# Blocks 0 to 2 of a four-block model in one structure with one set of PSUM banks, with the work between the attentions issued as steps among them

## The chip, the cores and the metric

The kernel runs on one core of one Trainium2 chip. The metric is the device time of one execution in microseconds. Before the change it is 3795.54 us, the median of three runs (3782.44 to 3795.83). The program is written in a tile language: the author allocates named tiles in pools, and a scheduler at build time gives them addresses, adds the semaphore waits and fixes the order of the instructions on each engine by its own estimate and by priority, which is the order in the program text. Where a matmul is pinned (`keep_in_program_order`), TensorE issues it in the order of the text.

## The reference, cut to what matters

Four residual blocks follow each other on x, of shape [4 batches, 1024 tokens, 128 channels]. Each computes `xn = layernorm(x); s = attn(xn); g = silu(ffn(xn)); x = x + s * g`.

- Block 0: attention of 16 heads of size 8 with rotary positions and a window of 250 keys; as ffn an RWKV channel mix: two blends of each token with the one before it, `r = sigmoid(xr @ W_r)`, `k = relu(xk @ W_k)**2`, `ffn = r * (k @ W_v)`.
- Block 1: causal attention; as ffn a mixture of 8 experts of which each token keeps its best two, hidden size 256, with gelu. All experts are computed for all tokens, and gates that are zero or not weigh them.
- Block 2: a whole transformer layer as attention (layernorm, full attention with rotary positions, `x + attn`, layernorm, an FFN of hidden size 512 with relu); as ffn a mixture of 8 experts of which each token uses one, with at most 80 tokens per expert over the whole input, so the place of a token among its expert's tokens depends on all batches.
- Block 3: a Mamba-like layer as attention and two layers of local attention as ffn. The change leaves its arithmetic alone.

Everything in blocks 0 and 1 and in block 2's attention is independent between the four batches. Only block 2's routing and its experts see all batches at once.

## The kernel before, in words

x, the normed x and s lie in SBUF as 32 tiles of 128 tokens (`k.x`, `k.xn`, `k.s`), and the normed x also turned, channels by tokens (`k.xT`). `tile_blocks` calls `_block0`, `_block1`, `_block2` and `_block3` one after the other. Each of the first three opens PSUM banks of its own by `_banks`, once for the norms, once for the attention and once for the ffn, and does each phase for all four batches before it goes on:

1. `_ln_to_fm` (L549): layernorm of a batch (`_layernorm_parts`: statistics and scaling on VectorE, the power -0.5 on GpSimd, L72) and eight transposes on TensorE (L88), for four batches.
2. `_attention` (L121). A unit is one batch and four heads, 16 units in all. `project` computes q and k, applies rotary positions, splits them in three bf16 parts on GpSimd (`_split`, L104 to L107) and stores them to DRAM; `load` reads them back in another layout (q9, k9). `maxima` computes all scores once to get each row's maximum: a matmul into `max_ps` and a reduction on VectorE (L288). `attend` computes the scores again into `sc`, applies exp on ScalarE (L363), masks on GpSimd where needed (L332), and multiplies by the values into `o_ps`. Its PSUM set is two pairs of banks (tag "m": projections, `max_ps`), three single banks (tag "s": `sc` and all transposes) and one bank (tag "o": `o_ps`).
   The order of work is written out by hand. Before the first `attend`, batch 0 is projected, units 0 and 1 are loaded, the maxima of unit 0 are taken and the first two fifths of those of unit 1. Then, for each unit, `_interleave` mixes as streams the maxima of the coming units, the blocks of this unit's `attend`, and a third of the projections of the next batch. All TensorE work here is pinned.
3. The ffn for all batches: the channel mix in L580 to L604; the router, the gates and the experts of block 1 in L640 to L690, with all expert weights resident; in block 2 the FFN (L745 to L772) and `_experts` (L817: a one-hot matrix per tile, dispatch matmuls, experts, combine).
4. `silu`, `g = s * g` on GpSimd (L98) and `x += g` on VectorE (L99).

All loads and stores are issued by SyncE in one in-order queue; an issue that waits holds up those behind it. Block 3's first weights (`_weights3`) are loaded into a pool on the right side of SBUF that is opened before block 2.

Of the kernel before, what the change touches and what calls it, by code (L numbers as in the profile page):

```python
# [29 lines left out]
P = 128  # L30
# [18 lines left out]
@contextmanager  # L49
def _banks(k):  # L50

    with k.tc.tile_pool(name="ps", bufs=2, space=PSUM) as k.ps:
        yield


# [26 lines left out]

def _to_fm(k, src, dst, scale=None, bias=None):

    nc, n = k.nc, src.shape[1]
    ps = k.ps.tile([P, 4, P], F32, tag="mx", name="tr_ps")
    for i in range(n):
        nc.tensor.transpose(ps[:, i, :], src[:, i, :], k.ident)  # L88
    flat = ps[:, :n, :].rearrange("p a b -> p (a b)")
    if scale is None:  # L90
        nc.scalar.copy(dst, flat)
    else:
        nc.vector.tensor_scalar(dst, flat, scale, bias, ALU.mult, ALU.add)


def _add_product(k, s, g, x):

    k.nc.gpsimd.tensor_tensor(g, s, g, ALU.mult)  # L98
    k.nc.vector.tensor_tensor(x, x, g, ALU.add)  # L99
# [10 lines left out]
def _interleave(*streams):  # L110

    total = max(len(s) for s in streams)
    done = [0] * len(streams)
    for step in range(total):
        for i, s in enumerate(streams):
            while done[i] < len(s) and done[i] * total < (step + 1) * len(s):
                s[done[i]]()
                done[i] += 1


def _attention(k, pool, mode, xT, w, out, rope=None):  # L121
# [22 lines left out]
    ps2 = lambda name: k.ps.tile([P, 2, 512], F32, tag="m", name=name, bufs=2)  # L144
    ps1 = lambda name: k.ps.tile([P, 512], F32, tag="s", name=name, bufs=3)
    pin = k.tc.keep_in_program_order

    def matmul(*args, **kw):
        pin(nc.tensor.matmul(*args, **kw))  # L149

    def transpose(*args):
        pin(nc.tensor.transpose(*args))

    def project(b):
# [5 lines left out]
        def half(what, hf):  # L160
            cols = slice(512 * hf, 512 * hf + 512)

            def step():
# [22 lines left out]
                if hf == 1:  # L186
                    parts = pool.tile([P, 3, T], BF16, tag="parts", name=f"{what}p", bufs=2)
                    _split(nc, nc.gpsimd, d, parts, d)
                    dense[what, "parts"] = parts
# [50 lines left out]
    def maxima(n):  # L240

        q9, k9 = units[n]
        neg = pool.tile([P, 4, NT], F32, tag="neg", name="neg", bufs=3)

        def tile_of(parts):


            def step():
                ps = ps2("max_ps")
# [51 lines left out]
        held = {}  # L301

        def split():
            held["p"] = parts = pool.tile([P, 3, 4 * NT], BF16, tag="negp", name="negp", bufs=2)
# [3 lines left out]
        def spread():  # L308
            parts = held.pop("p")
            tp = k.ps.tile([12 * NT, P], BF16, tag="s", name="neg_ps", bufs=3)  # L310
# [31 lines left out]
    def attend(n):  # L342
# [5 lines left out]
        def weights(hf, n):  # L348
            kt, c0, width = blocks[hf][n]
            off = kt * P - c0  # L350
            held[hf, n] = pt = pool.tile([P, 4, 384 if mode == "window" else 512], F32, tag="pt", name="pt", bufs=1 + lag)

            def pair(p2):
                for j in (2 * p2, 2 * p2 + 1):
# [8 lines left out]
                    nc.scalar.activation(pt[:, j, :width], sc[:, :width], AF.Exp, scale=scale)  # L363


                two = slice(2 * p2, 2 * p2 + 2)
                if mode != "full" and off >= 0:
                    keep(pt[:, two, off : off + P], 1, 0)
                edge = max(0, off + CONTEXT)
                if mode == "window" and width > edge:  # L370
                    keep(pt[:, two, edge:width], -1, off + CONTEXT - 1 - edge)
# [3 lines left out]
        def values(hf, n):  # L375
# [6 lines left out]
            o, pt = held["o", hf], held.pop((hf, n))  # L382
            for j in range(4):
# [4 lines left out]
                    rhs=pt[:, j, :width],  # L388
# [9 lines left out]
        def normalize(hf):  # L398
            os = held.pop(("os", hf))
            ot = k.ps.tile([P, 4, 4, 32], F32, tag="s", name="ot", bufs=3)  # L400
# [62 lines left out]

    def run(steps):
        for step in steps:
            step()

    run(project(0))
    load(0)
    load(1)  # L470
    steps, ending = maxima(0)
    run(steps + ending)
    steps, ending = maxima(1)
    lead = 2 * len(steps) // 5
    run(steps[:lead])
    late = []
    for n, (b, g) in enumerate(order):
        if g == 0:
            dense["at", b] = pool.tile([P, NT, H, HD], F32, tag="at", name="at", bufs=2)
        ahead = []  # L480
        if n + 1 < N:

            ahead = steps[lead:] + ending[:1]
            last = ending[1]
            if n + 2 < N:
                load(n + 2)
                steps, ending = maxima(n + 2)
                ahead += steps[: lead - 2] + [last] + steps[lead - 2 : lead]
            else:
                ahead.append(last)  # L490
        weights, closing = attend(n)
        streams = [ahead, weights]
        if b + 1 < B and g < 3:
            if g == 0:
                coming = project(b + 1)
            streams.append((coming[:3], coming[3:7], coming[7:])[g])
        if late:

            for i in range(lag + 1):
                weights.insert(1 + 2 * i, late[i])  # L500
            for i, step in enumerate(late[lag + 1 :]):
                weights.insert(min(len(weights), 2 * lag + 4 + 3 * i), step)
        _interleave(*streams)
        late = closing + (finish(b) if g == 3 else [])
    run(late)


def _first_max(k, pool, lg, name):

    nc = k.nc  # L510
    full = [P, NTILE, E8]
    m = pool.tile([P, NTILE, 1], F32, tag="fm_m", name="fm_m")
# [5 lines left out]
    i = pool.tile([P, NTILE, 1], F32, tag="fm_i", name="fm_i")  # L518
# [6 lines left out]
def _softmax8(k, pool, lg, m, scale):  # L525

    nc = k.nc
    full = [P, NTILE, E8]
# [3 lines left out]
    z = pool.tile([P, NTILE, 1], F32, tag="sm_z", name="sm_z")  # L532
# [6 lines left out]
def _router(k, pool, xT, wg, bg):  # L539

    nc = k.nc
    ps = k.ps.tile([P, NTILE, E8], F32, tag="ms", name="rt_ps", bufs=1)
    for n in range(NTILE):
        b, t0 = n // NT, 1 + (n % NT) * P
        nc.tensor.matmul(ps[:, n, :], lhsT=xT[:, b, t0 : t0 + P], rhs=wg, start=True, stop=True)
    lg = pool.tile([P, NTILE, E8], F32, tag="lg", name="lg")
    nc.vector.tensor_tensor(lg, ps, bg.unsqueeze(1).to_broadcast([P, NTILE, E8]), ALU.add)
    return lg


def _ln_to_fm(k, pool, src, xT, keep=None, scale=None, bias=None):

    for b in range(B):
        if keep is None:
            xn = pool.tile([P, NT, C], F32, tag="ln_x", name="ln_x", bufs=2)
        else:
            xn = keep[:, b * NT : b * NT + NT, :]
        _layernorm(k, src[:, b * NT : b * NT + NT, :], xn)
        for i in range(2):
            c0 = 1 + 512 * i  # L560
            _to_fm(k, xn[:, 4 * i : 4 * i + 4, :], xT[:, b, c0 : c0 + 512], scale, bias)


def _block0(k, t):
    nc = k.nc
    x, xT, s, g = k.x, k.xT, k.s, k.xn
    with k.tc.tile_pool(name="w0", bufs=1) as wp:
        w0 = wp.tile([P, 9 * P + 2], F32, name="w0")
        nc.sync.dma_start(w0, t["w0"])
        names = ("q", "qs", "k", "ks", "v", "o", "wr", "wk", "wv")  # L570
        w = {n: w0[:, i * P : i * P + P] for i, n in enumerate(names)}
        mu_r, mu_k = w0[:, 9 * P : 9 * P + 1], w0[:, 9 * P + 1 : 9 * P + 2]
        with k.tc.tile_pool(name="a0", bufs=1) as pool:
            rope = pool.tile([P, 2, T], F32, name="rope")
            nc.sync.dma_start(rope, t["rope"][:, 0])
            with _banks(k):
                _ln_to_fm(k, pool, x, xT)
            with _banks(k):
                _attention(k, pool, "window", xT, {n: w[n] for n in names[:6]}, s, rope)
        with k.tc.tile_pool(name="f0", bufs=2) as pool, _banks(k):  # L580
            for n in range(8):
                b, o = n // 2, 512 * (n % 2)
                cur, prev = xT[:, b, o + 1 : o + 513], xT[:, b, o : o + 512]
                dx = pool.tile([P, 512], F32, name="dx")
                nc.gpsimd.tensor_tensor(dx, cur, prev, ALU.subtract)
                xr = pool.tile([P, 512], F32, name="xr")
                nc.vector.scalar_tensor_tensor(xr, dx, mu_r, prev, ALU.mult, ALU.add)
                xk = pool.tile([P, 512], F32, name="xk")
                nc.vector.scalar_tensor_tensor(xk, dx, mu_k, prev, ALU.mult, ALU.add)
                kp = k.ps.tile([P, 512], F32, tag="ms", name="kp", bufs=1)  # L590
                nc.tensor.matmul(kp, lhsT=w["wk"], rhs=xk, start=True, stop=True)
                ka = pool.tile([P, 512], F32, name="ka")
                nc.scalar.activation(ka, kp, AF.Relu)
                nc.gpsimd.tensor_tensor(ka, ka, ka, ALU.mult)
                rv = k.ps.tile([P, 2, 4, P], F32, tag="sc", name="rv")
                for c in range(4):
                    cs = slice(c * P, c * P + P)
# [1234 lines left out]
```

## Time and profile before

The profiled execution took 3796.72 us; its trace spans 3795.0 us. The median of the three other runs is 3795.54 us, so a sum made on the trace is 1 to 2 us short of either.

| engine | busy in the span | instructions |
|---|---|---|
| TensorE, matmuls (PE) | 3349.1 us, 88% | 25426 |
| TensorE, weight loads (PEld) | 1858.6 us, 49% | 25428 |
| VectorE (DVE) | 2502.8 us, 66% | 4932 |
| ScalarE (ACT) | 1966.8 us, 52% | 4192 |
| GpSimd (POOL) | 1362.9 us, 36% | 1887 |

The mean granted TensorE clock is 0.916. The DMA queue of SyncE carries 118.98 MB; its packets take 13.7% of the 16 DMA engines' time. The profile's chain of work that ended last reaches back only to about 2750 us, into block 3, so it says nothing on the blocks before it.

How to read it: busy shares over the whole span average stages with different limits. The stages here can be cut by the first and last matmul of a kind. First scores of an attention: 104, 678 and 1655 us; last output projection: 533, 1221 and 2484 us; first matmul of block 3: 2744 us. A window table by these cuts, with each engine's busy time and the granted clock, is what the prediction works on. A fp32 matmul appears as two instructions.

### The profile page before, as it was taken

Reading aid. Unit: us, or ns where it says so; the run is one execution under the profiler, and the core shown is the slowest. Engines: PE = TensorE matmul, PEld = TensorE weight load, DVE = VectorE, ACT = ScalarE, POOL = GpSimd, SP = SyncE. Lnnn points to the kernel's source line nnn. Section 1 sums busy time; section 2 is a strip of 40 time slices with the busy share of each in tenths; the row PEclk is TensorE's granted clock in tenths of the full one; section 3 lists DMA queues with packets and bytes.
Section 4 is the critical chain, followed back from the end, with each engine's and each line's share of the span. In section 5 each row is a group of like instructions: output and inputs, shape, how many; then the busy total and the mean of one; then the engine's idle time right before and its main releaser. Section 6 shows DMA issues by size and latency. Waiting matters only on the chain. (4 is left out here: it accounts for less than half of the span.)

```text
span 3795.0 us, 65266 instructions
## 1 busy us (share of the span) xinstructions
PE 3349.1 (88%) x25426; PEld 1858.6 (49%) x25428; DVE 2502.8 (66%) x4932; ACT 1966.8 (52%) x4192; POOL 1362.9 (36%) x1887
## 2 busy tenths in 40 slices
PE   3999984999999999389999999989779999999898
PEld 2554542444444676123333233257756676666665
DVE  5666655777773434388778688444478888877785
ACT  0444551566565443036666666731056656665674
POOL 3555463322321001421110300010186677656663
PEclk7999995999998998579999999999589999999999
DMA  3222202212220000201111111010021001001110
GB/s 81 62 63 56 51 3 68 56 40 43 56 39 15 1 1 13 56 19 35 35 34 26 30 26 26 1 51 6 17 61 21 18 21 29 20 21 22 28 27 22
DMA packets 110419, 123.14 MB, mean 32 GB/s; under 512 B 77336, under 2 KB 89888, under 8 KB 102432
## 3 DMA queue, kind: packets, MB, share of 16 engines
q1 hardware_dynamic: 110112, 118.98, 13.7%
q8 instruction: 201, 3.29, 0.4%
q14 instruction: 106, 0.87, 0.1%
HBM read 77.91 MB, written 23.07 MB: 27 GB/s over the span
## 5 line engine op out<-in xcount | busy, mean ns | idle before, releaser
L363 ACT ACTIVATE pt<-sc 128x512 f32<-128x512 f32 (+3 forms) x2432 | 1073.1, 512 | 856.5 <-PE sc L149 848.2
L288 DVE TENSOR_REDUCE neg<-max_ps 128x1 f32<-128x1024 f32 (+6 forms) x1088 | 1171.5, 1102 | 485.2 <-PE max_ps L149 469.1
L149 PE MATMUL max_ps<-k,q 72*128 72x512 bf16 (+3 forms) x2304 | 683.0, 366 | 140.1 <-DMA k<-kx 104.7
L149 PE MATMUL sc<-q,k 75*128 75x512 bf16 (+3 forms) x2432 | 646.8, 343 | 45.9 <-ACT pt L363 35.0
L149 PE MATMUL o_ps<-pt,va 128*32 128x512 f32 (+3 forms) x4864 | 561.8, 528 | 4.6 <-POOL pt L332 4.4
L332 POOL TENSOR_SCALAR_AFFINE_SELECT pt<-pt 128x256 f32<-128x256 f32 (+2 forms) x768 | 290.6, 394 | 512.1 <-ACT pt L363 506.1
L149 PEld LDWEIGHTS <-q 72*128 72x128 bf16 x2304 | 227.4, 101 | 413.1 <-issue 289.7
L149 PEld LDWEIGHTS <-k 75*128 75x128 bf16 x2432 | 183.0, 98 | 496.6 <-issue 399.2
L104 POOL CAST negp<-neg 128x32 bf16<-128x32 f32 x48 | 10.0, 209 | 643.8 <-DVE neg L288 643.7
L1384 ACT ACTIVATE pr<-lsc,nb,r 128x128 f32<-128x128 f32 x512 | 202.2, 475 | 62.1 <-DVE nb L1376 58.6
L1305 POOL TENSOR_TENSOR qn<-qn,rot 128x512 f32<-128x512 f32 x128 | 164.5, 1291 | 137.3 <-DVE rot L1297 122.6
L1314 POOL TENSOR_TENSOR rn<-ss,neghalf 128x16 f32<-128x16 f32 x64 | 188.8, 2949 | 69.7 <-DVE ss L1312 60.2
L149 PEld LDWEIGHTS o_ps<-pt,va 128*32 128x32 f32 x4864 | 100.9, 109 | 204.8 <-issue 162.1
L149 PEld LDWEIGHTS <-ident 128*128 128x128 bf16 x1472 | 151.8, 104 | 89.0 <-issue 23.8
L679 PEld LDWEIGHTS op<-ew,h 128*128 128x128 f32 x1024 | 134.1, 195 | 66.5 <-ACT h L675 34.8
L675 ACT ACTIVATE h<-hp,eb 128x512 f32<-128x512 f32 x128 | 87.5, 687 | 133.9 <-PE hp L668 133.9
L688 DVE SCALAR_TENSOR_TENSOR xn<-op,gates,xn 128x128 f32<-128x128 f32 x256 | 72.0, 344 | 125.0 <-PE op L679 122.7
L1222 PE MATMUL qk_ps<-wqkv,hT 128*128 128x512 f32 x256 | 135.2, 612 | 21.7 <-DVE hT L1268 7.3
L679 PE MATMUL op<-ew,h 128*128 128x128 f32 x1024 | 138.4, 279 | 4.6 <-ACT h L675 4.6
L149 PE MATMUL max_ps<-mask_window,ident 128*128 128x134 bf16 (+2 forms) x960 | 139.2, 228 | 0.0
L668 PE MATMUL hp<-xT,ew 128*128 128x512 f32 x256 | 134.5, 608 | 0.4 <-ACT h L675 0.4
L395 DVE COPY os<-o_ps 128x512 f32<-128x512 f32 x96 | 65.5, 682 | 85.3 <-PE o_ps L149 85.3
(355 smaller groups left out, 5742.4 us busy)
## 6 DMA issues: line engine op xcount, KB each, us to landing
q<-qx SPq DMA_DIRECT2D x144, 192.0 KB
k<-kx SPq DMA_DIRECT2D x432, 64.0 KB
va<-vb SPq DMA_DIRECT2D x120, 128.0 KB
qx<-qp SPq DMA_DIRECT2D x12, 768.0 KB
kx<-kp SPq DMA_DIRECT2D x12, 768.0 KB
mw<-in_e2w_dram SPq DMA_DIRECT2D x2, 2048.0 KB
q<-negr SPq DMA_DIRECT2D x144, 8.0 KB
x<-in_x_dram SPq DMA_DIRECT2D x4, 512.0 KB
```

The lines of the kernel that those rows point to most:

```text
L149: pin(nc.tensor.matmul(*args, **kw))
L288: nc.vector.tensor_reduce(neg[:, j0 : j0 + m, qt0], of, AX.X, ALU.max, negate=True)
L332: nc.gpsimd.affine_select(out=pt, in_=pt, pattern=[[0, 2], [step, pt.shape[2]]], compare_op=ALU.is_ge, fill=0.0, base=base, channel_multip ...
L363: nc.scalar.activation(pt[:, j, :width], sc[:, :width], AF.Exp, scale=scale)
L668: nc.tensor.matmul(hp[:, hh, :], lhsT=ew1[:, e, hh * P : hh * P + P], rhs=xT[:, b, o : o + 512], start=True, stop=True,)
L675: nc.scalar.activation(h[:, hh, :], hp[:, hh, :], AF.Gelu, bias=eb1[:, e, hh : hh + 1])
L679: nc.tensor.matmul(op[:, c, :], lhsT=h[:, hh, c * P : c * P + P], rhs=ew2[:, e, hh, :], start=hh == 0, stop=hh == 1,)
L688: nc.vector.scalar_tensor_tensor(to, op[:, c, :], gates[:, 4 * n + c, e : e + 1], to, ALU.mult, ALU.add)
L1222: pin(nc.tensor.matmul(*args, **kw))
L1305: nc.gpsimd.tensor_tensor(qn[:, i], qn[:, i], rot, ALU.add)
L1314: nc.gpsimd.tensor_tensor(rn, ss.rearrange("p w h -> p (w h)"), k.neghalf[:, : 2 * NH], ALU.pow)
L1384: nc.scalar.activation(t.pr[:, h, :], t.sc[r][:, c, :], AF.Exp, bias=t.nb[r][:, c : c + 1], scale=t.r8[:, h : h + 1])
```

## The change

- One function `_blocks012` holds blocks 0 to 2 with one PSUM pool that is open throughout: the attention's set ("m", "s", "o"). All other matmuls of the three blocks up to block 2's FFN use its tags and are pinned in program order too (helpers `_mm`, `_tr`, `_ps1`, `_ps2`).
- `_attention` no longer runs by itself. It returns `begin`, a list of steps up to the first `attend`, and `rest(post, aside)`. `rest` runs the units and has one more stream, `aside`: `post(b-1)` gives the steps that follow batch b-1's attention, and they are spread over the units 1 to 3 of batch b. What `post` gives for the last batch is returned.
- The phases became lists of small steps per batch or half batch: `_norm_steps`, `_fm_steps`, `_update_steps`, `_channel_mix`, `_silu_steps`, `_moe`, `_gating`, `_ffn`. They are placed so: the norms of batches 1 to 3 and the whole channel mix beside block 0's `begin`; x update, norm, router and gates of block 1 for batches 0 to 2 inside block 0's attention; those of batch 3 and the experts of block 1 for batches 0 to 2 beside block 1's `begin`; x update, norm, router logits and second norm of block 2 for batches 0 to 2 inside block 1's attention; the experts for batch 3 beside block 2's `begin`; batch 3's update and norms and the FFN of batches 0 to 2 inside block 2's attention; the FFN of batch 3 after it, then block 2's routing, then the experts as before.
- The exp tile `pt` is allocated per pair of heads (five buffers of two heads, tag "pt") instead of per block (2 or 3 buffers of four heads), and other steps take their scratch from the same five buffers; `ln_x` and `fm` share the two buffers of tag "os".
- Block 1's expert weights are no longer resident: `fetch(e)` loads one expert's 256 KB, for each batch anew, into three rotating buffers, from the SyncE queue.
- Block 2's expert weights are loaded after its attention as before, but the FFN of only one batch lies between. `_weights3` moved behind blocks 0 to 2.

The diff, cut to its core:

```diff
             def pair(p2):
+                held[hf, n, p2] = pt = pool.tile([P, 2, 512], F32, tag="pt", name="pt", bufs=5)
...
+    begin = project(0) + [lambda: load(0), lambda: load(1)] + steps + ending
+    begin += steps[:lead]
+    def rest(post, aside=[]):
...
+            if b and g == 1:
+                aside += post(b - 1)
+            share = -(-len(aside) // (4 - g))
+            if share and (b == 0 or g):
+                streams.append(aside[:share])
+                aside = aside[share:]
+            _interleave(*streams)
+            late = closing + (finish(b) if g == 3 else [])
+        _run(late)
+        return post(B - 1)
+    return begin, rest
...
+def _moe(k, pool, wp, t, gates, eb1, eb2, b):
+    def fetch(e):
+        ews[e] = ew = wp.tile([P, 512], F32, tag="ew", name="ew", bufs=3)
+        nc.sync.dma_start(ew[:, 0:256], t["e1w1"][:, e])
+        nc.sync.dma_start(ew[:, 256:512].rearrange("p (h c) -> p h c", h=2), t["e1w2"][:, e])
...
+    for i in range(len(jobs) + 1):
+        if i < len(jobs):
+            e, n = jobs[i]
+            if n == 0 and e + 2 < E8:
+                steps.append(lambda e=e: fetch(e + 2))
+            steps.append(lambda e=e, n=n: hidden(e, n))
+        if i:
+            steps.append(lambda i=i: output(*jobs[i - 1]))
...
+def _ffn(k, pool, w, b):
+    def output(n, f2):
+        h = held.pop(("h", n, f2))
+        if f2 == 0:
+            held["op", n] = _ps1(k, "op2", (P, 4, P))
...
+    steps = [lambda: nc.gpsimd.tensor_tensor(s[:, a, :], s[:, a, :], k.xn[:, a, :], ALU.add), None]
+    for i in range(2):
+        steps += [lambda i=i: norm(i), None, lambda i=i: held.pop(("n", i))(), lambda i=i: to_fm(i)]
...
+                begin, rest = _attention(k, pool, "window", xT, wa, s, rope)
+                _run(normed[0])
+                mix = [_channel_mix(k, pool, w, mu_r, mu_k, n) for n in range(2 * B)]
+                for b in range(B):
+                    other += (normed[b + 1] if b + 1 < B else []) + mix[2 * b] + mix[2 * b + 1]
+                _interleave(other + _silu_steps(k, range(B)), begin)
+                last = rest(lambda b: to_block1(b, wp, wp))
...
+        begin, rest = _attention(k, pool, "causal", xT, wa, s)
+        _interleave(moe(pool, 0) + moe(pool, 1) + moe(pool, 2), last, begin)
+        last = rest(lambda b: to_block2(b, pool) if b < B - 1 else [])
...
+        begin, rest = _attention(k, pool, "full", xT, wb, s, rope)
+        _interleave(moe(pool, B - 1), begin)
+        _run(rest(lambda b: _ffn(k, pool, wb, b), to_block2(B - 1, pool)))
...
-    _block0(k, t)
-    _block1(k, t)
+    _blocks012(k, t, lambda b: _norm3(k, b))
+    stream.close()
     with tc.tile_pool(name="early3", bufs=1, side="right") as wp:
         _weights3(k, t, wp)
-        _block2(k, t, lambda b: _norm3(k, b))
-        stream.close()
         _block3(k, t, out)
```

## The prediction

> **What bounds the kernel now.** I read the slices first, then a window table cut by stages, then TensorE's waits in the stages with low busy time, then the groups of instructions for durations. In the slices, the digits under PE and the granted clock fall together at the joints between the attentions:
>
> ```profile
> PE   3999984999999999389999999989779999999898
> PEclk7999995999998998579999999999589999999999
> ```
>
> The second view is the window table (us, busy of PE, PEld, DVE, ACT, POOL, then clock, DMA share, GB/s):
>
> ```profile
> 0.00:104.00 104.00, 43.57 (x202) 27.48 (x202) 56.16 (x133) 7.14 (x11) 36.73 (x37) 0.76 0.33 79
> 104.00:533.00 429.00, 394.60 (x3593) 215.65 (x3591) 259.10 (x368) 216.29 (x646) 235.18 (x596) 0.96 0.24 51
> 533.00:678.00 145.00, 74.51 (x320) 46.24 (x321) 90.54 (x168) 32.22 (x41) 62.91 (x41) 0.62 0.21 50
> 678.00:1221.00 543.00, 516.57 (x3775) 222.00 (x3774) 371.52 (x473) 333.31 (x780) 154.67 (x340) 0.98 0.19 40
> 1221.00:1655.00 434.00, 346.78 (x1699) 229.99 (x1698) 192.60 (x585) 120.48 (x169) 65.05 (x43) 0.79 0.08 20
> 1655.00:2484.00 829.00, 795.05 (x4341) 255.72 (x4340) 607.36 (x661) 549.14 (x1048) 107.14 (x125) 0.98 0.12 25
> 2484.00:2744.00 260.00, 229.72 (x1188) 184.00 (x1187) 113.25 (x283) 41.25 (x98) 33.73 (x26) 0.79 0.06 25
> 2744.00:3795.00 1051.00, 948.26 (x10318) 677.52 (x10320) 812.24 (x2266) 667.00 (x1400) 667.52 (x679) 0.95 0.11 27
> ```
>
> I call the rows A (start), B (window attention), C (joint), D (causal attention), E (joint), F (full attention), G (block 2's FFN and experts) and H (block 3). In B, D and F TensorE is busy 92 to 96% at clock 0.96 to 0.98. That this is its peak shows in the timeline of F: a block of `attend` with its maxima takes 2.83 us, and its matmuls start every 0.22 us without a gap, while DVE waits 0.48 us per block for `max_ps`. So in B, D and F every matmul put in costs its own time, and other engines have room. In A, C and parts of E TensorE waits. The third view cuts E and G finer:
>
> ```profile
> 1234.00:1487.00 253.00, 245.72 (x1378) 174.96 (x1377) 101.47 (x360) 108.30 (x150) 11.97 (x6) 0.97 0.00 1
> 1487.00:1546.00 59.00, 32.50 (x135) 25.77 (x133) 37.32 (x170) 7.23 (x11) 11.02 (x7) 0.53 0.06 20
> 1546.00:1601.00 55.00, 11.77 (x33) 6.01 (x34) 2.17 (x9) 4.95 (x8) 39.94 (x25) 0.59 0.27 75
> 1601.00:1655.00 54.00, 44.57 (x90) 11.21 (x89) 50.66 (x45) 0.00 (x0) 0.91 (x4) 0.50 0.20 38
> 2485.00:2565.00 80.00, 72.47 (x369) 50.78 (x370) 35.43 (x87) 21.88 (x32) 16.55 (x13) 0.89 0.15 60
> ```
>
> The experts of block 1 (first row) are bound by TensorE: 253 us for 8 half batches, 31.6 us each. Then come 59 us of update, norms and routing, 55 us in which GpSimd prepares q and k and TensorE does nearly nothing, and 54 us of first maxima bound by DVE. The fourth view names the waits of E:
>
> ```profile
> PE max_ps L149 <- DMA k<-kx: 42.7, 1, 42.7
> PE tr_ps L88 <- DVE ln_x L76: 22.0, 6, 7.0
> ```
>
> **The change part by part.** TensorE's work stays: both programs have the same number of matmuls. What can go is waiting and half clock at the joints. I place the moved work with the built program's order of instructions, which has no times.
>
> A, 104 us. Batch 0's projection no longer waits for the transposes of four batches (it starts at 37.4 us now), but on GpSimd the five memsets (3 x 3.5 and 2 x 1.2 us) now stand ahead of the first norm's power (first issued at 7.7 us now, then about 17), and five blends, two squares and two or three powers (1.0 to 1.4 us each) stand inside and between the two splits. I get the k store at 50 us instead of 59.8, and the first maxima 10 us earlier. The channel mix then adds its DVE work, 16 blends at 1.3 us and 8 products at 0.7, 26 us, in a stage where DVE is busy 56 of 104. The three prefetched experts and block 1's weights, 1.1 MB, go through SyncE ahead of the q store, in the time it waits for the split. I take +6 us; between -10 (all hidden) and +25 (all DVE work exposed).
>
> B. For batches 0 to 2 it takes 16 transposes and 8 logit matmuls for each of 3 batches: only 8 of the transposes a batch are B's (the block 1 norm), at 0.16 us (`ot`, 60.8 us for 384), and the logits at 0.2 (`rt_ps`, 26.2 us for 128): 3 us a batch, +9. GpSimd gets the 2.4 us product (L98) and four powers a batch in front of the masks; it is busy 235 of 429 and the masks have two blocks of lead, so I cost it at nothing; with the lead gone it is 3 x 7 us.
>
> C. The 145 us go: the mix, update, norm and the 28.5 us wait for k. In come the experts of three batches, 6 x 31.6 = 190 us, and the TensorE work of `begin`: 8 projection matmuls at 0.53 us, 16 of the values at 0.14, maxima of 30 steps at about 0.5 and 3 us for batch 3: 25 us. The preparation of k (about 40 us) lies under the eleven expert steps that stand before the first maximum. 215 us, +70.
>
> D. Two sets of 8 transposes and 8 logits a batch, 4.2 us, three batches: 13; `fm` and `ln_x` share two buffers with `os`, 1 us. +14.
>
> E, 434 us. 253 us of experts become one batch, 63; update, norms and routing leave. But the 55 us stay: the built order puts only the projections, two hidden and one output step of the experts ahead of block 2's first `max_ps`, and GpSimd's memsets, rotary products and splits stand as before. TensorE so still waits some 37 us there. After it, 44 maxima (DVE 50.7 us) and the remaining 14 jobs run together: TensorE 19 + 60 us, DVE 51 + 20, so 80, and 7 us to the first scores. 55 + 80 + 7 = 142, -292.
>
> F. The FFN of a batch costs 33.0/4 + 34.2/4 = 16.8 us (L752, L763) and 1.3 of transposes: 54 us for three. Batch 3's norms and logits 4. `op2` holds one of the three `sc` banks between its two halves, for about 2.3 blocks, six times: the fourth score then waits for the exp before, at most 0.5 us a block, 5 us. DVE gets norms in bursts of 1.4 to 1.7 us, where its slack per block is 0.48 us: about 13 bursts at 0.7 us, 9 us. Relu brings no more table loads on ScalarE: 110 in the whole program, 108 before. +72, F 901.
>
> Here a rule of the Trainium skill speaks against the change: "TensorE: Matmul & The Clock Gate", section "A second HAM failure mode: psum-queue depth-cycling", tells of a kernel in which cycling through PSUM banks makes TensorE idle so often in small gaps that its clock swings between half and full. By it, the nine units with an FFN (520 us) at a mean clock of 0.75 would take 173 us more, and the kernel 3816. By the row, F cycles through just these banks already and has clock 0.98. I take the row.
>
> G, 260 us. Of the 80 us of FFN, one batch stays, exposed: 8 us to its first matmul, 17 of TensorE, 5 for half clock and the last sum: 30. Routing (chain of 14 us in E now) stands wholly after it: 15. The rest from the first dispatch (2558.6 us) takes 185 less some 4 that overlapped with the FFN, and 3 for a cold start. 229, -31. The 4 MB of expert weights now wait for attention buffers, but landed in 12 us before and have 80; block 3's 1.2 MB have 200. If not hidden, +12 and +5.
>
> H stays at 1051.
>
> Sum: 3795 + 6 + 9 + 70 + 14 - 292 + 72 - 31 = 3643 of span. The profiled execution was 1 us above the median and 2 above its span, so 3643 to 3644; I say 3643.
>
> **Rivals.**
> - *Shared banks and buffers loosen the attentions.* If in the nine units that carry an FFN each of the 16 blocks takes 3.3 instead of 2.83 us, +68 us less the 14 already counted, and half that once more in B and D (masks behind GpSimd's products): 3643 + 54 + 20 = 3717. For it: the stalls on `max_ps` by DVE that F already has, 13.5 us. Against: even with some 45 us of norms DVE would be busy 652 of 901 us of F, 72%.
> - *More cover than I count.* TensorE at half clock in G's combine (clock 0.74 from 2565 on) could come out warm, -40, or GpSimd's 55 us could begin inside D, -20: 3585. Against: the built order keeps both as they are.
> - *SyncE's queue starves the experts; slower than before.* Each of the 29 later fetches waits in order for its buffer and behind q/k loads, which held the queue for 19 to 22 us at each `begin`. An expert's two jobs take TensorE 7.9 us. Over 3814 us needs 171 us lost, 5.9 us per fetch, so it decides when a fetch cycle takes over 13.8 us. Against: a fetch is issued two experts ahead, about 14 us, and 256 KB are small beside 4 MB in 12 us.
> - *The steps end up where they were.* The scheduler could have undone it, about 3790. The built order shows the steps inside the attentions.
>
> **How the numbers follow.** 0.64 for the sum (own range 3605 to 3685), 0.17 for loosened attentions (3717), 0.13 for more cover (3585), 0.03 for SyncE and 0.01 for the clock rule (both slower), 0.02 for no change. A measurement of this kernel can tell about 0.5% from no change, 19 us. Faster 0.64 + 0.17 + 0.13 = 0.94, same 0.02, slower 0.04. The range 3585 to 3715 leaves out the slow tail and about half of the second case.
>
> **What would show it.** In the changed profile: clock near 1 from A's end to F's end but for one hole of about 40 us before block 2's first `max_ps`, with a wait for k by DMA there and none in C; C bound by TensorE at about 215 us; F 70 us longer with no new wait over 10 us; after F a stretch of 45 us with a poor TensorE. The prediction is wrong if waits of `hp` for DMA appear (SyncE), if waits of `sc` for exp grow beyond 30 us in F, or if A passes 130 us.

## The result, and the profile after

The changed kernel takes 3757.60 us (median of 4 runs, 3753.68 to 3758.84); the kernel before, beside it, 3789.25 us (4 runs, 3782.44 to 3795.83). The ratio is 0.9915, with a 95% interval of 0.989 to 0.994: 32 us faster, where the prediction said 3643 us. The sign was right, and four fifths of the gain did not come. In the later groups of runs the kernel before took 3779 to 3783 us (medians, in the table of the experiments); against those the gain is 21 to 25 us. The profiled execution of after spans 3752.0 us.

The slices of after, TensorE's busy tenths and granted clock:

```profile
PE   5989988999889895899999999878879999989898
PEclk7999999999989987999999999986589999999999
```

Of the two deep dips of before, the 4 at slice 7 is gone, and of the 3 at slice 17 a 5 at slice 16 is left. But inside the attentions slices 3, 11, 12 and 14 fall from 9 to 8, and the clock is low in the four slices 27 to 30, in two before.

The window table of after, cut by the same events as before (columns: us, busy PE, PEld, DVE, ACT, POOL, clock, DMA share, GB/s):

```profile
0.00:112.50 112.50, 63.08 (x346) 45.23 (x347) 70.57 (x161) 30.87 (x39) 56.25 (x57) 0.82 0.35 90
112.50:562.90 450.40, 409.22 (x3667) 225.58 (x3665) 289.57 (x515) 221.58 (x656) 250.07 (x605) 0.94 0.22 47
562.90:790.40 227.50, 210.93 (x1203) 148.74 (x1203) 99.31 (x284) 79.14 (x118) 31.60 (x20) 0.95 0.19 55
790.40:1399.40 609.00, 549.47 (x3874) 239.13 (x3872) 408.29 (x644) 341.89 (x790) 173.14 (x355) 0.93 0.16 35
1399.40:1551.90 152.50, 100.48 (x467) 60.92 (x467) 72.94 (x120) 29.97 (x45) 42.70 (x30) 0.84 0.19 50
1551.90:2457.70 905.80, 854.89 (x4638) 290.89 (x4636) 635.96 (x765) 570.28 (x1075) 121.80 (x137) 0.98 0.11 23
2457.70:2700.00 242.30, 200.67 (x925) 168.34 (x925) 101.43 (x269) 25.71 (x76) 25.95 (x21) 0.67 0.08 32
2700.00:3752.00 1052.00, 950.64 (x10318) 678.20 (x10320) 812.19 (x2266) 667.25 (x1398) 667.29 (x679) 0.95 0.11 27
```

Set against the predicted lengths:

| stage | before | predicted | after | miss |
|---|---|---|---|---|
| A start | 104 | 110 | 112.5 | +2.5 |
| B window attention | 429 | 438 | 450.4 | +12.4 |
| C joint | 145 | 215 | 227.5 | +12.5 |
| D causal attention | 543 | 557 | 609.0 | +52.0 |
| E joint | 434 | 142 | 152.5 | +10.5 |
| F full attention | 829 | 901 | 905.8 | +4.8 |
| G block 2's FFN, experts | 260 | 229 | 242.3 | +13.3 |
| H block 3 | 1051 | 1051 | 1052.0 | +1.0 |

The misses add up to 109 us, half of it in D, where the clock fell from 0.98 to 0.93. TensorE's waits in D (us in total, times, longest) show what is new; before, `max_ps` waited for VectorE there 0.2 us in all, and `proj_ps` not at all:

```profile
PE proj_ps L78 <- DVE neg L331: 17.6, 2, 8.8
PE sc L78 <- ACT pt L404: 15.5, 39, 2.9
PE max_ps L78 <- DVE neg L331: 10.6, 5, 8.8
```

Among these are three waits of 8.8 us, two of `proj_ps` and one of `max_ps`: one for the norms of each of the batches 0 to 2. The timeline of TensorE around the first (start, length, instruction, and in brackets the idle time before it):

```profile
955.99 0.60 PE L82 MATMUL ot<-ident,os 128*128 128x128 f32 x4
965.41 2.08 PE L78 MATMUL proj_ps<-xT,w 128*128 128x512 f32 x2 [8.81 <-DVE neg L331]
```

and VectorE's in the same stretch, of which only the ends are shown:

```profile
955.35 1.22 DVE L138 TENSOR_TENSOR x<-x,xn 128x1024 f32<-128x1024 f32 x1 [1.88 <-POOL xn L136]
956.60 0.49 DVE L60 BATCH_NORM_STATS2 ln_st<-x 128x6 f32<-128x128 f32 x2
...
964.59 0.17 DVE L63 TENSOR_SCALAR ln_ve<-ln_mv 128x4 f32<-128x4 f32 x1
964.67 1.82 DVE L331 TENSOR_REDUCE neg<-max_ps 128x4 f32<-128x512 f32 x2
```

What to see: between the update of x and the next maximum VectorE does the statistics of eight tiles, the eight applications and the statistics of the second norm, 44 instructions and 9.3 us with the update, without reading `max_ps`. Both "m" buffers hold unread maxima, so TensorE, whose order is pinned, stands at the next instruction that needs one. The program text has these norms as separate steps spread over the units 1 to 3 of the next batch; but only TensorE is pinned, and the scheduler pulled VectorE's part forward into unit 0, to where its inputs are ready. After the hole the clock stays at half until about 969 us, as two rows of a window table show:

```profile
964.00:968.00 4.00, 2.59 (x5) 1.06 (x6) 2.91 (x9) 0.42 (x1) 1.95 (x2) 0.50 0.01 2
968.00:972.00 4.00, 4.00 (x24) 1.39 (x22) 1.79 (x2) 2.79 (x6) 0.00 (x0) 0.88 0.00 0
```

### The profile page after: what moved, and what is told of

It reads as the page before. It is cut to its first block, busy times and chain, and to the rows that moved or that the text cites. A ratio compares the mean times of both kernels' runs of the same rounds, so it can differ in the third digit from the quotient of the medians.

```text
span 3752.0 us, 66158 instructions
## 1 busy us (share of the span) xinstructions
PE 3339.4 (89%) x25426; PEld 1857.0 (49%) x25428; DVE 2490.3 (66%) x5021; ACT 1966.7 (52%) x4197; POOL 1368.8 (36%) x1903
## 5 line engine op out<-in xcount | busy, mean ns | idle before, releaser
L78 PE MATMUL max_ps<-k,q 72*128 72x512 bf16 (+3 forms) x2304 | 654.1, 353 | 79.6 <-DVE neg L331 31.6
L78 PE MATMUL sc<-q,k 75*128 75x512 bf16 (+3 forms) x2432 | 664.8, 347 | 65.6 <-ACT pt L404 47.7
L78 PE MATMUL o_ps<-pt,va 128*32 128x512 f32 (+3 forms) x4864 | 570.1, 537 | 2.9 <-POOL pt L374 1.8
L78 PEld LDWEIGHTS op<-ew,h 128*128 128x128 f32 x1024 | 124.1, 193 | 20.2 <-issue 17.5
L1028 PE MATMUL comb_ps<-eo,ohT 80*128 80x128 f32 x512 | 115.5, 420 | 14.2 <-DVE ohT L1018 13.7
L78 PE MATMUL op<-ew,h 128*128 128x128 f32 x1024 | 126.0, 277 | 0.0
```

Of the source, the lines that this page charges most:

```text
L78: k.tc.keep_in_program_order(k.nc.tensor.matmul(*args, **kw))
L1028: nc.tensor.matmul(gp[:, c, :], lhsT=ohT[:, e, c * P : c * P + P], rhs=eo[:, e, :], start=e == 0, stop=e == E8 - 1,)
```

## The experiments

The table lists all of them; the kernel before ran beside each group (medians 3778.91, 3782.81 and 3781.90 us).

| run | median us | ratio to before, 95% interval |
|---|---|---|
| e1_spread | 3701.18 | 0.9789 (0.9749 to 0.9829) |
| e2_d_away | 3745.95 | 0.9904 (0.9873 to 0.9934) |
| e3_efirst | 3682.46 | 0.9733 (0.9691 to 0.9776) |
| e4_ffn_away | 3739.00 | 0.9885 (0.9844 to 0.9925) |
| e5_wide | 3687.83 | 0.9753 (0.9722 to 0.9784) |
| e6_rows | 3664.33 | 0.9683 (0.9656 to 0.9711) |
| e7_vmem | 3696.11 | 0.9774 (0.9747 to 0.9801) |
| e8_all | 3649.82 | 0.9650 (0.9625 to 0.9675) |
| e9_best | 3632.37 | 0.9611 (0.9597 to 0.9626) |
| e10_before_rows | 3764.17 | 0.9956 (0.9942 to 0.9970) |
| e11_before_pt | 3807.37 | 1.0082 (1.0050 to 1.0114) |

A reading used below is the length of each of the 16 units of an attention, from its first exp to that of the next unit, less the same unit of before. For D, in us, four units (g = 0 to 3) to a batch:

```
            batch 0           batch 1           batch 2           batch 3
after     +5.7 +.3 +.4 +.4  +11.8 +.3 +7.0 +1.6  +12.7 -.8 +4.3 +1.9  +11.7 +.2 +4.9 +2.2
e1_spread +9.1 +.3 +.4 +.3    +.6 +.9 +4.4 +2.2    +.3 -.2 +5.3 +2.5    +.3 +.8 +6.7 -2.1
e2_d_away +9.2 +.6 +.8 +.3   +1.1 +.3  +.4  +.3    -.1 -.8  +.4  +.3    +.3 +.2 +7.5 -4.9
e5_wide   +5.1 +.5 +.3 +.3    +.9 +.9 +3.2 +2.1    +.4 -.2 +3.1 +2.6    +.3 +.8 +2.3 -3.3
```

**e1: the norms pinned on VectorE.** In `_layernorm_parts` and the update of x, from block 0's attention to the end of block 2's:

```diff
-        nc.vector.bn_stats(out=st[:, i, :], in_=src[:, i, :])
+        pin(nc.vector.bn_stats(out=st[:, i, :], in_=src[:, i, :]))
...
-        lambda: k.nc.vector.tensor_tensor(x, x, g, ALU.add),
+        lambda: k.tc.keep_in_program_order(k.nc.vector.tensor_tensor(x, x, g, ALU.add)),
```

> The update of x and all statistics and applications of the norms in blocks 0 to 2 are pinned to their written place on VectorE; nothing else changes. Theory 1 (a run of norms on VectorE): in the changed kernel's causal attention VectorE does an update, 16 statistics and 8 applications in one run of 9 us ahead of the next maximum, so TensorE stands for 8.8 us at a bank that holds an unread maximum and then runs some 5 us at half clock, three times. Pinned, the three units that were 11.7 to 12.7 us longer than before come down to 1 to 3 us longer, the three holes of 8.8 us go, the causal attention falls from 609 us to about 577, the window attention by 3 to 8, and the whole to about 3715. Theory 2 (the moved steps' TensorE work, the shared banks or the half-block weight buffers): the same steps and banks are still there, so the causal attention stays within 8 us of 609 and the time within 10 us of 3757.

The window table of e1, rows B, D and G, and TensorE's waits in D for VectorE's maxima:

```profile
111.40:544.60 433.20, 397.03 (x3667) 220.22 (x3665) 291.53 (x515) 221.25 (x656) 250.28 (x605) 0.97 0.23 49
...
771.70:1347.60 575.90, 541.04 (x3874) 237.21 (x3872) 408.30 (x644) 341.29 (x790) 175.71 (x355) 0.96 0.18 37
...
2401.70:2647.70 246.00, 201.49 (x924) 168.85 (x924) 102.39 (x269) 25.71 (x76) 26.22 (x21) 0.67 0.08 31
PE max_ps L81 <- DVE neg L334: 1.8, 4, 0.5
```

VectorE does the same 644 instructions in 408.3 us in D, yet D is 33 us shorter; B is 17 shorter, F 7. The span is 53 us shorter (3699.0). The three units of D that were 12 us too long are within 0.6 us of before, and the three waits of 8.8 us are gone. Theory 1 is shown: the order on VectorE cost about half of what was missing. It cost more than expected (the whole was put at 3715, B at 3 to 8). How much of B's 17 us is due to it is loose: in six traces with pinned norms and logits of 8 columns (e1 to e4, e6, e7) B takes 430 to 444 us, as its half-clock spells lie differently, while D with its steps stays at 569 to 581. Theory 2 is left with the rest of D, 576 for 557.

**e2: the steps taken out of D.** From e1:

```diff
-        last = rest(lambda b: to_block2(b, pool) if b < B - 1 else [])
+        _run(rest(lambda b: []))
+        for b in range(B - 1):
+            _run(to_block2(b, pool))
```

> As the pinned kernel, and the update, norms, transposes and logits of batches 0 to 2 for block 2 run after the causal attention instead of inside it. Theory 1: what is left inside is the attention alone, with its shared banks and half-block buffers, and every unit of it is within 1.5 us of the kernel before, but the first (cold start): 543 to 553 us from first score to the end. The steps then stand exposed behind it, about 20 us a batch, 55 to 65 us, so the time is 20 to 30 us above that of the pinned kernel. Theory 2 (banks, half-block buffers): the attention without the steps is still over 565 us.

D is 560 us by the stage cuts, a little more than expected: 9.2 us lie in the first unit, which starts with 17 us at half clock, and 2.6 in the last two. All others are within 1.1 us of before, so shared banks are no rival for D's 609. Behind D the joint grew by 66 us (155 to 221), more than the expected 55 to 65, and the whole by 45, where 20 to 30 were expected. Inside, in e1, the same steps cost 16 us.

**e3: batch 3's experts earlier at the joint E.** From e1, with m the steps of `moe(pool, B - 1)`:

```diff
-        _interleave(moe(pool, B - 1), begin)
+        _interleave(m[:12], begin[:4])
+        _interleave(m[12:34], begin[4:11])
+        _interleave(m[34:], begin[11:])
```

> As the pinned kernel, and at the joint before block 2's attention the first 34 of the steps of batch 3's experts are issued among the projections, ahead of the first maximum, instead of evenly over all of the attention's beginning. If the joint (152 us) is set by TensorE's order, in which the experts stand behind maxima that wait for GpSimd's q and k, the two holes of 16 and 18 us and their half clock fill up, and the joint takes 105 to 120 us: 35 to 45 us less than the pinned kernel. If it is set by GpSimd's 43 us and VectorE's maxima, 50 us, in a chain, what is moved is idle either way and the joint stays above 140.

E took 145.9 us for 155.4, above the 140 of the second reading. TensorE's two large holes shrank from 36 us to 9.5, but the first `max_ps` came 67 us after D's end in place of 57, so behind it 79 us passed in place of 99. SyncE's queue shows why k came late: the fetches of the experts, which wait for a buffer that TensorE still reads, now stand among k's loads (the last column counts the issues):

```profile
1398.64 0.36 SPq L650 DMA_DIRECT2D ew<-in_e1w_dram  x1
1399.04 0.43 SPq L651 DMA_DIRECT2D ew<-in_e1w_dram  x1
1399.51 0.67 SPq L280 DMA_DIRECT2D k<-kx  x2
1406.54 0.36 SPq L650 DMA_DIRECT2D ew<-in_e1w_dram  x1
1406.94 1.47 SPq L651 DMA_DIRECT2D ew<-in_e1w_dram  x1
1408.45 0.67 SPq L280 DMA_DIRECT2D k<-kx  x2
```

The edit so moved two things at once, and the gain behind the first maximum was lost ahead of it. Of the 19 us by which the median is under e1's, 13 lie in G, where the clock came back for a while; the intervals of the two overlap.

**e4: the FFN out of F.** From e1, `_ffn` of all batches after the attention.

> As the pinned kernel, and block 2's FFN of all four batches runs after the full attention, as before the change, instead of three of them inside it. If TensorE binds in the full attention, the FFN costs there what it costs anywhere: the attention falls by 60 to 70 us, the stage after it grows by 55 to 70, and the time is within 10 us of the pinned kernel. If the FFN fills idle time inside the attention, the time rises by 40 us or more.

F fell by 59 us (898.7 to 840.0), and the stage after it grew by 101 (246 to 347), so the time rose by 38: by its total this is nearest the second reading. But the 101 us are four FFNs one after the other, each with two waits of some 4.3 us for a norm and 17 to 20 us at half clock, in which TensorE was busy 11 to 12. In the kernel before, where the batches overlapped, all four took 80. Inside F a batch costs 59/3 = 19.6 us, as much as it did there. By these sums, and not by e4's total, the move gained nothing by itself.

**e5: logits with 128 columns.** In e1's trace, short spells of half clock start where TensorE is busy. Cut in windows of 2 us, they begin in D at 1008, 1152, 1292 and 1312 us, and in B at 520. Batches of router logits end 0.5 to 2.5 us ahead of all of these but the one at 1312; four other batches, at 308, 421, 717 and 1623 us, have no spell behind them, and three spells of 3.4 us in B, at 152, 261 and 374 us, have no logits ahead of them. What precedes the first is, in the timeline and in two rows of a window table:

```profile
1003.69 1.16 PE L81 MATMUL v_ps<-w,xT 128*128 128x128 f32 x8
1004.68 1.85 PE L81 MATMUL rt_ps<-w,fm 128*128 128x8 f32 x16
```

```profile
1004.00:1008.00 4.00, 4.00 (x38) 3.05 (x37) 2.46 (x7) 0.80 (x3) 0.00 (x0) 1.00 0.02 4
1008.00:1012.00 4.00, 3.66 (x19) 1.10 (x18) 1.59 (x3) 1.88 (x4) 0.91 (x4) 0.61 0.00 0
```

Eight router logits (16 instructions) multiply whole 128x128 tiles with 8 columns. Each takes the same 0.112 us from start to start as the `v_ps` matmuls with 128 columns just before them. The edit, from e1, streams 128 columns of the weight tile, of which the last 8 are the logits, in two halves:

```diff
-        _mm(k, ps[:, i, :], lhsT=of(i), rhs=wg, start=True, stop=True)
+            _mm(k, ps[:, i, :], lhsT=of(4 * h + i), rhs=wg, start=True, stop=True)
...
-                    _logits(k, lg[0], of, w1[:, 4 * P + 2 : 4 * P + 10], r1[:, 2 * P : 2 * P + E8])
+                    _logits(k, lg[0], of, w1[:, 3 * P + 10 : 4 * P + 10], r1[:, 2 * P : 2 * P + E8])
...
```

> As the pinned kernel, and the router logits of blocks 1 and 2 multiply with 128 columns of the weight tile, of which the last 8 are the logits, in place of 8 columns; their matmuls follow each other every 0.112 us in both cases. Theory 3 (narrow matmuls let the clock drop): in the pinned kernel a half-clock spell of 4 to 8 us begins within 2.5 us after each such batch of logits in the attentions (1008, 1152, 1292, 1312 us), though TensorE is busy. With 128 columns these spells go, and each third unit of a batch in the causal attention, 4.4 to 6.7 us longer than before, comes down by 2 to 3.5 us; the whole gains 8 to 20 us. If the spells have another cause, they stay at these places, and the time is within 5 us of the pinned kernel's 3701.

The row of D in e5:

```profile
762.80:1326.20 563.40, 527.52 (x3874) 233.29 (x3871) 408.37 (x647) 341.04 (x790) 175.72 (x355) 0.99 0.18 38
```

D has the same 3874 matmuls, and the clock is 0.99 in place of 0.96. Behind none of the eight batches of logits does a spell begin any more; the one that was at 1312 us is left, 3 us long, at 1294. The third units came down by 1.2, 2.2 and 4.4 us, B by 11 and D by 12.5. The median is 13 under e1's, while the intervals overlap; the spans differ by 21. The other traces agree: with 8 columns a spell begins within 2.5 us behind the same three batches in D in e3, e4 and e6, and behind one of them in e7; with 128, in e8 and e9, behind none. So theory 3 is shown at the places. Its size in time is loose, 13 to 21 us: the three spells in B without logits are gone as well, which the theory doesn't explain (B takes 422 to 425 us in e5, e8 and e9), and in e8 D takes 575 us, as its last spell is 24 us long. Why only four of eight batches had a spell behind them is open.

**e6: the combine over 128 partitions.** G was 13 us over the prediction, all of it in block 2's combine, which took 126.5 us before (26 at full clock, then 100.5 at 0.53) and now takes 140 at 0.52. Two rows of before and one of after:

```profile
2618.00:2644.00 26.00, 23.52 (x207) 22.98 (x205) 13.18 (x39) 4.46 (x13) 6.44 (x5) 1.00 0.05 21
2644.00:2744.50 100.50, 83.46 (x349) 75.87 (x349) 39.89 (x113) 5.70 (x20) 10.40 (x9) 0.53 0.03 11
2560.00:2700.00 140.00, 125.09 (x569) 119.46 (x569) 63.13 (x166) 9.12 (x32) 17.05 (x13) 0.52 0.03 12
```

It contracts over the 80 tokens of an expert. From e1:

```diff
-    eo = pool.tile([CAP, E8, P], F32, name="eo", bufs=1)
+    eo = pool.tile([P, E8, P], F32, name="eo", bufs=1)
+    nc.gpsimd.memset(eo, 0.0)
...
-        ohT = pool.tile([CAP, E8, 512], F32, name="ohT", bufs=2)
+        ohT = pool.tile([P, E8, 512], F32, name="ohT", bufs=2)
...
```

> As the pinned kernel, and the combine of block 2's experts contracts over 128 partitions, of which the last 48 hold zeros in the experts' output, in place of 80. The number of matmuls and columns stays. If the half clock of the combine (148 us, 73 us lost) comes from rows that are not used, the clock comes back to near 1 and the stage from the end of the attention to block 3 falls from 246 us to 190 to 210. If it comes from the waits for VectorE or from the weight loads ahead of each matmul, the stage stays within 5 us.

The row of G in e6, to set beside e1's above:

```profile
2412.70:2616.80 204.10, 154.17 (x924) 122.97 (x924) 102.55 (x269) 25.70 (x76) 26.57 (x22) 0.87 0.10 38
```

With 924 matmuls in both, busy TensorE falls from 201 to 154 us and the clock rises from 0.67 to 0.87; the stage is 42 us shorter, and the time 1% better than e1's. The waits of the combine for VectorE are still there (20.0 us in all, 13.7 in e1). That the empty rows let the clock drop is shown for this stage.

**e7: constants set by VectorE in blocks 1 and 2.**

```diff
-        nc.gpsimd.memset(t_[64:96], 1.0)
+        (nc.gpsimd if mode == "window" else nc.vector).memset(t_[64:96], 1.0)
...
```

> As the pinned kernel, and the constants of q, k and the values of the causal and the full attention are set by VectorE in place of GpSimd. At the joint before block 2 GpSimd's five memsets (13 us) stand ahead of the rotary products, and k's load ends the wait there. If GpSimd's chain sets the joint, k comes 10 to 12 us earlier and the joint of 155 us falls by 8 to 15; the time falls by as much. If the maxima on VectorE and the half clock behind the hole set it, the joint stays above 150.

E fell by 8 us, to 147.1, and its first `max_ps` came 49 us after D's end in place of 57. But C, where VectorE has the experts' sums to do, grew by 10.6: near its start TensorE waits 15.9 us for VectorE, and 24 us run at half clock. The total is not told from e1's.

**e8: all edits at once.** The three edits, and 24 of the experts' steps among the projections.

> The pinned kernel with all three edits at once, and 24 of batch 3's expert steps among the projections at the joint before block 2. If the parts add up, 3701 less what each of the three gave alone, less 10 to 20 for the experts: 3610 to 3670 us.

It lies inside the range. C kept the loss of e7 (238.5 us), and E gained nothing over e7 (151 for 147).

**e9: the parts that helped.** e1 with wide logits and the combine over 128 partitions, VectorE's constants in the full attention alone, and the experts in the changed kernel's order.

> The pinned kernel with the wide logits, the combine over 128 partitions, and the constants set by VectorE in the full attention only; batch 3's experts in the changed kernel's order. The gains of the parts lie in different stages (13 in the window and causal attentions, 42 at the end, 8 at the joint before block 2; the joint before block 1 keeps its 227), so they should add: 3701 - 13 - 37 - 8 = 3643, 3630 to 3655. If they don't add, it stays above 3660.

The gains add up: A to H take 111, 424, 230, 566, 147, 898, 204 and 1050 us. At 3632 us this version beats both kernels. That it comes near the predicted 3643 is not the prediction's sum come true: against the predicted lengths, B and G are 14 and 25 us shorter, and C, D and E 15, 9 and 5 longer.

**e10: the combine's edit in the kernel before.** The same edit as in e6.

> The kernel before with one edit: block 2's combine contracts over 128 partitions, 48 of them zeros, in place of 80. Its combine ran the first 26 us at full clock and then 49 us of it were lost to half clock. If unused rows let the clock drop whatever runs ahead of it, the stage falls from 260 us to about 225 and the time by 25 to 35. If the half clock belongs to what the change did to this stage, the time stays within 5 us.

The stage fell by 20 us (260 to 240) and the time by 18, less than expected but beyond the interval: the half clock is not of the change's making. In this combine 37 us still run at half clock, in spells of 3 to 10 us; before it was 94.

**e11: the half-block weights in the kernel before.** The edit of `pt` from the change, alone.

> The kernel before with one part of the change alone: the attention weights in five buffers of half a block, in place of three whole blocks (window, causal) or two (full). If the smaller lead cost something, the window and causal units would be longer than before by several per cent, some 20 us in all. By the causal units without moved steps, which were 0.3 us longer than before in the changed kernel, the whole is within 8 us.

Slower by 0.8%, 25 us in the medians: nearer the first reading by its total, nearer the second by its units, of which none is several per cent longer. In D almost every unit is 0.3 to 0.4 us longer than before, in F 0.4 to 0.6, in B mostly 0.2 to 0.3: some 16 us over the 48 units. The other 9 us are not placed; the two traces differ by 4 us only, as their half-clock spells lie differently. The trace of a block in F shows where the units lose: ScalarE now has a separate wait instruction ahead of the third exp of most blocks, for the second half's buffer (its trace has 1254 such instructions, 736 before). That exp starts 0.06 us behind it, and ScalarE's idle time in brackets is 0.04 us longer, first in e11, then before:

```profile
1777.36 2.07 ACT L363 ACTIVATE pt<-sc 128x512 f32<-128x512 f32 x4 [0.81 <-PE sc L149]
1781.35 2.06 ACT L363 ACTIVATE pt<-sc 128x512 f32<-128x512 f32 x4 [0.77 <-PE sc L149]
```

The fourth score, which waits for the bank of the first exp of this chain, follows 0.04 us later: 16 x 0.04 = 0.6 us a unit. That this instruction is the cause is read from the trace and was not tried apart from the smaller buffers. In the changed kernel the units without moved steps show the same +0.3 in D, and in e4's F +0.5.

## Why the prediction failed, step by step

**The step that failed is D**, put as "Two sets of 8 transposes and 8 logits a batch, 4.2 us, three batches: 13; `fm` and `ln_x` share two buffers with `os`, 1 us." It counts TensorE's share and one buffer and gives VectorE's norms nothing, on the ground that "other engines have room". On the average they had (VectorE busy 408 of 609 us), but not in the place where the scheduler put them. VectorE's order in the trace has, per batch, the update, 44 norm instructions and only then the next maximum. For F the prediction counted such bursts, of 1.4 to 1.7 us; for D it counted none. Cost, by e1: 33 us in D, 7 in F, and 17 in B, which the other pinned traces put at 6 to 21. The rest of D's miss is the logits' spells (12.5 us by e5), a slow first unit (5 to 9 us longer) and the half-block weights.

**Half clock was priced only at the joints it looked at.** In "What would show it" the clock was to be near 1 from A's end to F's end but for one hole. Behind each 8.8 us hole 3.6 to 6.6 us run at half clock (until 969, 1129 and 1283 us), 2 to 3 us of full-speed work lost; the hole itself is the larger part of the 11.7 to 12.7 us. The moved logits brought their spells into the attentions: 13 to 21 us, by e5. For F the weighing was right: the row's 0.98 held. The mean clock of 0.75 set against it was an estimate, the middle of half and full; the section cited there gives no size.

**G**: "The rest from the first dispatch (2558.6 us) takes 185 less some 4". The combine alone took 13.5 us more than before, at half clock from near its start. e6 and e10 show what lets the clock drop; why before's combine ran its first 26 us at full clock is open.

**C**, 12.5 over: one wait of 8.0 us of an expert for ScalarE's copy of k, which itself waits for GpSimd's split of q, and three half-clock spells of 7 us each. In e1's trace two of these start within 2 us of the turned gates and the bias products, which have 8 columns or 8 rows. That fits e5 and e6, but no run tries it.

**E**, 10.5 over: the hole was as predicted (55 us to the first maximum, measured 56; 34.5 us idle). Behind it 97 us passed in place of 87. e7 shows that GpSimd's constants stand in the chain ahead of the first maximum: without them it comes 8 us earlier, and E falls by 8. Whether TensorE's order binds behind it is open, as e3 moved the experts and held up k's loads at once.

**The half-block weights** were not in the sum at all. They cost 0.2 to 0.6 us a unit (e11), some 16 us over 48 units. In F this doesn't show in the miss, as the FFN there was counted 9 us too high.

**A, F and H** were right within 5 us, F in part by luck: 54 us of TensorE and 14 of stalls and bursts were predicted for its FFN, and e4 measured 59 in all, which left room for the half-block weights and the norms' order.

Of the rivals, "the steps end up where they were" (about 3790) came nearest in time. In part it is what happened: the scheduler did move steps, but only VectorE's, and forward into unit 0. "Shared banks and buffers loosen the attentions" (3717; half of its 54 is 27, where it adds 20) was wrong in its mechanism: TensorE waited 1.5 us for GpSimd's masks in B and 14.6 us for exp in F (10.9 before), and in e2 D's units have before's length with the banks shared. For "more cover", e6 gives the 40 us of a warm combine, but by filled rows and not by cover. SyncE did not starve the experts in the changed kernel; in e3 it did harm for 10 us. None of the three signs of being wrong appeared (no `hp` waits for DMA, `sc` waits 14.6 us for exp in F, A takes 112.5 us), and none of them looked at D.

Together: with norms, logits and combine mended, and the constants moved, e9 is at 3632. What the prediction missed was not the work it counted but the order on an unpinned engine and the clock. A rule of the Trainium skill, "TensorE: Matmul & The Clock Gate", section "Why this matters for your kernels", asks for no idle gap above some 3 us between bursts. It covers the three holes, which the clock followed to half, but not the spells in which TensorE was busy 7.66 of 8 us (e1's two rows), nor a combine busy 125 of 140 us at clock 0.52. There the measurement decides.

## What to carry to other kernels

When steps are moved into a stage, read the built order of every engine that is not pinned: the scheduler here gathered small instructions where their inputs were ready, and a run of them longer than the buffers' lead stopped the pinned engine, however much room VectorE had on the average. Where TensorE already bound the stage, as in F, moving the FFN in gained nothing (19.6 us a batch, 20 outside); what counted were the holes that were filled or removed. Watch the clock after short, narrow or partly empty matmuls too, and try padding them to the full tile where that costs no time.

## What the runs showed of the hardware that was not expected

- Sixteen instructions of 8 columns in 1.7 us, with TensorE busy, were followed within 2.5 us, in four of eight places, by 3 to 14 us at half clock (e1). With 128 columns and the same spacing of 0.112 us no such spell was left (e5, e8, e9; D's clock 0.96 in e1 and 0.99 in e5).
- In a combine over 80 of 128 rows the clock was 0.52 for 140 us while TensorE was busy 125 of them; with 48 rows of zeros added the clock of its stage rose from 0.67 to 0.87 (e1, e6), and the stage took 204 us in place of 246. The kernel before ran the first 26 us of the same combine at full clock, so unused rows don't bring half clock at once.
- The wait for a half block's buffer is a separate instruction on ScalarE (1254 of them in e11's trace, 736 before); 0.06 us for it, in a chain of exps that TensorE waits for, stands beside 0.04 us more per block.
